# Padding the small SBUF tiles of a graph-network kernel to 128 bytes a partition

## The chip, the cores and the metric

One NeuronCore of a Trainium2 chip. The metric is the device time of one execution in microseconds (us), as the median of several executions. The kernel before takes 1516.46 us, the median of three runs from 1515.87 to 1516.89.

## The reference

A graph layer over 6250 nodes of 64 features and 200000 edges that are sorted by target node, all in float32:

```
w     = silu(edge_attr_32 @ W1 + b1) @ W2 + b2            # per edge: 32 -> 64 -> 9
h_src = x[src]                                            # per edge: a row of 64
msg   = einsum('ef,em,fmg->eg', h_src, edge_attr_9 * w, W_tp)
agg   = segment_sum(msg, dst, num_segments=6250) / sqrt(16)
gamma, beta = split(silu(node_vec[:, None] @ Wn1 + bn1) @ Wn2 + bn2, 2)
y     = x + agg * (1 + gamma) + beta
out   = (y - mean(y)) / sqrt(var(y) + 1e-5)               # over the 64 features
```

## The kernel before

Edges go in tiles of 128, one edge a partition, and 16 tiles make a group: 1563 tiles, 98 groups (`NBLK`). The loop over the groups is written out by hand under a manual schedule, so each engine gets its instructions in the order of the source. In turn `i` the kernel finishes group `i`, prepares group `i + 1` and starts on group `i + 2`.

**Source rows.** For most tiles of a group the rows `x[src]` come by indirect DMA, one for each tile, issued by POOL (`gather`, L93), six groups ahead, into one of seven `hs` buffers. Every fourth group has one tile that SP loads row by row instead (`load_rows`, L104 and L109). The last four tiles of a group (three in every fourth) need no DMA: `pick` forms their rows on TensorE. The node table stands in SBUF as `xs[0]` and `xs[1]`, two float32r halves of every value, 49 node rows a partition in seven slices of 7 x 64 numbers. A one-hot `hot_k` marks the partition and the slice of each edge's node (DVE, L479). Fourteen matmuls (seven slices, two halves) accumulate in `px` (PE, L494: stationary `hot_k[:, h]`, 128x128; moving `xs[i][:, h]`, 448 float32r a partition). DVE selects one row in seven (`xm`, L503) and sums it into `hs` (L505).

**Edge weights and sums.** `hidden` (L422, L430) and `second` (L439, L442) are the two-layer network on the edge attributes, and `weights` (L449, L455, L461) turns its result and spreads it over a window of seven nodes (`a`). `windows` (L527) multiplies rows by weights, ACT copies the result into `ztw` (L537), `project` (L573, L576, L579) multiplies by W_tp, and `place` and `bring` (L589, L595, L598, L606) add windows to nodes. `nodes` also holds the gate's matmul (L619), and `finish_nodes` (L710 to L725) the layer norm. A general path behind a flag is for other orders of edges; it is not entered with these inputs.

**SBUF.** Tiles come from pools, which lay their tiles one after the other in the order in which they are first asked for. In the program as built, every tile begins at a multiple of 32 bytes: a tile of 4 bytes a partition takes 32. So a small tile between two large ones moves the second by 32 bytes or not, by how many small ones stand ahead of it. These are the start addresses, as the remainder of a division by 64 and by 256 bytes; the offsets of the slices that the instructions address inside `xs`, `hot_k`, `ztw`, `ea`, `hs` and `c` are themselves multiples of 64:

```
tile (bytes a partition)                read or written at            before: mod 64, mod 256   after: mod 64, mod 256
ea, sh, kr, cb (first of each, loads)    L390, L392, L410, L354, L422    0, 128                      0, 0
hs (4096, seven buffers)                L93, L109, L505, L527           0, 128                      0, 0
st, p2s, a, r, c, carry, rt, yt (work)  L430 to L606                    0                           0
ident, ident2                           L449, L579, L606                0                           0
xs0, xs1 (12544 each)                   L494 moving                    32, 32                       0, 0
hot_k (3584, seven buffers)             L494 stationary, L479          32, 160                      0, 0
ztw (10240)                             L573 moving, L537              32                           0
wn2a, ht0, ht1                          L619 moving, stationary        32                           0
xm, y, sq, o                            L503, L505, L710 to L725       32                           0 (o, xm, y, sq)
gam, xb (12544 each)                    L239, L240, L710, L711         32                           0
```

Of the kernel before, what the change touches and what calls it, by code (L numbers as in the profile page):

```python
# [7 lines left out]
F32 = mybir.dt.float32  # L8
I32 = mybir.dt.int32
# [3 lines left out]
AF = mybir.ActivationFunctionType  # L13
# [3 lines left out]
P = 128  # L17
N, F, M, D, H, E = 6250, 64, 9, 32, 64, 200000
# [3 lines left out]
KB = 16  # L22
NBLK = (NT + KB - 1) // KB
W = 7
# [6 lines left out]
J = 7  # L31
# [26 lines left out]
    return min(KB, NT - g * KB)  # L58


@with_exitstack
def gnn_resnorm_kernel(ctx: ExitStack, tc: tile.TileContext, x, src, dst, dst_row, ea, sh, cn,
                       w1, b1, w2, b2, wtp, wn1, bn1, wn2, bn2, out):
    nc = tc.nc

    consts = ctx.enter_context(tc.tile_pool(name="consts", bufs=1))
# [2 lines left out]
    src_i = consts.tile([P, NBLK * KB], I32)  # L69
    dst_i = consts.tile([P, NBLK * KB], I32)  # L70
    w1bd = consts.tile([P, 2 * H], F32)
    b1c = consts.tile([P, 1], F32)
    w2bd = consts.tile([P, 2, M], F32)
    b2r = consts.tile([P, M], F32)
    wtc2 = consts.tile([P, 5, F], F32)
    flag_i = consts.tile([1, 1], I32)
    gam = consts.tile([P, NJ, F], F32)
    xb = consts.tile([P, NJ, F], F32)
    eps = consts.tile([P, 1], F32)

    with ExitStack() as fast:
        loads = fast.enter_context(tc.tile_pool(name="loads", bufs=3))
# [2 lines left out]
        keep = fast.enter_context(tc.tile_pool(name="keep", bufs=1))  # L85
# [5 lines left out]
        def gather(g):  # L91
            hs[g] = gath.tile([P, KB, F], F32, tag="hs", name=f"hs{g}")
            hs_dma[g] = [nc.gpsimd.indirect_dma_start(  # L93
                out=hs[g][:, t - g * KB, :], out_offset=None, in_=x,
                in_offset=bass.IndirectOffsetOnAxis(ap=src_i[:, t:t + 1], axis=0))
                for t in range(g * KB + (g in SPG), g * KB + tiles(g) - picked(g))]
# [14 lines left out]
        ident = keep.tile([P, P], F32)  # L111
        ident2 = keep.tile([P, F], F32)
        w2p = keep.tile([P, D], F32)
        b2c = keep.tile([P, 1], F32)
        xs = [keep.tile([P, J, F, J], F32R, name=f"xs{i}") for i in range(2)]
        wi = keep.tile([P, W], F32)
        nf = keep.tile([P, 2 * P], F32)
        lo = keep.tile([P, NBLK], F32)
        nk = keep.tile([P, J], F32)
        li = keep.tile([P, J], F32)  # L120
        ztw = keep.tile([P, 4 * 5 * KB * 8], F32)
        zt = ztw[:, 0:4 * 5 * KW].rearrange("p (a c k w) -> p a c k w", a=4, c=5, k=KB)
        rel = keep.tile([P, NBLK * KB], F32)
        nid = keep.tile([P, NBLK], F32)
        first_f = keep.tile([KB, NBLK], F32)
        bad = keep.tile([P, 4], F32)
        spare = keep.tile([P, 1], F32)
        ext = keep.tile([P, 4], F32)
        C = NBLK * Q
        jl = keep.tile([P, C], F32)  # L130
        kd = dram.tile([C, P], F16, name="kd")
        cn_d = dram.tile([P, NJ], F32, name="cn_d")
        cn_v = cn_d.rearrange("p j -> (p j)")
        wn1c = keep.tile([H, 1], F32)
        bn1c = keep.tile([H, 1], F32)
        wn2a = keep.tile([H + 1, 2 * F], F32)
        ht = [keep.tile([H + 1, 4, P], F32, name=f"ht{k}") for k in range(2)]

# [212 lines left out]
        def gate_load(j0):  # L351
            nj = min(4, NJ - j0)
            cb[j0] = loads.tile([H, 4, P], F32, tag="cb", name=f"cb{j0}", bufs=2)
            nc.sync.dma_start(cb[j0][:, :nj].rearrange("h j p -> h (j p)"), rows(cn_v[j0 * P:(j0 + nj) * P], H))  # L354
# [30 lines left out]
        def load(g, split=False):  # L385

            n = min(LB, NBLK - g)
            e = loads.tile([P, LB, KB * P // 4], F32, tag="ea", name=f"ea{g}")
            for a0, a1 in ((0, 1), (1, n)) if split else ((0, n),):
                nc.sync.dma_start(e[:, a0:a1, :], ea[g + a0:g + a1].rearrange("g p c -> p g c"))  # L390
            s = loads.tile([P, LB, KB, M], F32, tag="sh", name=f"sh{g}")
            nc.sync.dma_start(s[:, :n].rearrange("p g k m -> p g (k m)"), sh[g:g + n].rearrange("g p c -> p g c"))  # L392
            for i in range(n):
                ea_t[g + i] = e[:, i, :]
                sh_t[g + i] = s[:, i]

        def near(g):

            n = min(LB, NBLK - g)
            o = loads.tile([P, LB * KB, W], F32, tag="oh", name=f"oh{g}")  # L400
            nc.vector.tensor_tensor(
                o[:, :n * KB, :], rel[:, g * KB:(g + n) * KB].unsqueeze(2).to_broadcast([P, n * KB, W]),
                wi[:, None, :].to_broadcast([P, n * KB, W]), op=ALU.is_equal)
            for i in range(n):
                oh_t[g + i] = o[:, i * KB:(i + 1) * KB, :]

        def load_keys(g):
            n = min(LB, NBLK - g)
            kr = loads.tile([P, LB, Q, P], F16, tag="kr", name=f"kr{g}", bufs=2)
            nc.sync.dma_start(kr[:, 0:n].rearrange("p g t e -> p (g t e)"),  # L410
                              rows(kd[g * Q:(g + n) * Q, :].rearrange("c e -> (c e)"), P))
            for i in range(n):
                kr_t[g + i] = kr[:, i, Q - picked(g + i):, :]
# [56 lines left out]
        def keys(g):  # L470

            pk_t[g] = psum.tile([P, Q, P], F32, tag="r", name=f"pk{g}")
            nc.scalar.copy(pk_t[g][:, 0:picked(g), :], kr_t.pop(g))  # L473

        def hots(g, t0, t1):

            for t in range(t0, min(t1, picked(g))):
                hot_k[g, t] = late.tile([P, J, P], F32R, tag="hot_k", name=f"hot_k{g}_{t}", bufs=7)
                nc.vector.tensor_tensor(hot_k[g, t], pk_t[g][:, t, None, :].to_broadcast([P, J, P]),  # L479
                                        nk.unsqueeze(2).to_broadcast([P, J, P]), op=ALU.is_equal)  # L480
# [149 lines left out]
        with tc.manual_schedule(), tc.tile_pool(name="temp", bufs=1) as temp:  # L630
            setup(temp)

            for i in range(NBLK):
                if i + AHEAD < NBLK:
                    gather(i + AHEAD)
                while stores:
                    stores.pop(0)()
                if i % LB == 0 and i + LB < NBLK:
                    if i > 0:
                        load(i + LB)  # L640
                    near(i + LB)
                if i % LB == 1 and i + 1 + LB < NBLK:
                    load_keys(i + 1 + LB)
                if i % 4 == 3 and i + 1 < NJ:
                    gate_load(i + 1)
                for g in SPG:
                    if AHEAD - SPS < g - i <= AHEAD:
                        load_rows(g, (AHEAD - g + i) * SPR)
                more = []
                if i + 2 < NBLK:  # L650
                    keys(i + 2)
                    more = [lambda: hots(i + 2, 0, 2)]
                pick(i + 1, 0, [nodes(i), more])
                if i + 2 < NBLK:
                    hots(i + 2, 2, Q)
                if 56 <= i <= 58:
                    reach(i - 56)
                if i == 60:
                    reach_all()
                if i + 2 < NBLK:  # L660
                    hidden(i + 2)
                if i == NBLK - 2:
                    break
                second(i + 1)
                windows(i)
                turn = project(i // 2) if i % 2 == 1 else []
                if i % 4 == 1 and i - 1 < NJ:
                    gate_hidden(i - 1)
                pick(i + 1, 1, [weights(i + 1), turn])
                for t in range(2, Q):  # L670
                    pick(i + 1, t)

            g = NBLK - 1
            second(g)
            nc.scalar.activation(spare, eps, AF.Sqrt)
            pick(g, 1, [weights(g)])
            pick(g, 2)
            sums(g)
            windows(g - 1)
            pick(g, 3)  # L680
            marks(g // 2)
            turn = project(g // 2)
            windows(g, [ZT])
            ends = []
            for f in turn + place(g // 2, psum.tile([P, 2 * P], F32, tag="s", name="ps_l")):
                f()
            marks(NBLK // 2)
            for f in bring(NJ - 3, NJ - 1, psum.tile([P, FB, F], F32, tag="s", name="py_l"), ends):
                f()
            windows(g, [0])  # L690
            ends.pop()()
            project(NBLK // 2)
            ps = psum.tile([P, 2 * P], F32, tag="p1", name="ps_n")
            for f in place(NBLK // 2, ps) + bring(NJ - 1, NJ, psum.tile([P, 1, F], F32, tag="r", name="py_n")):
                f()
            while stores:
                stores.pop(0)()
# [206 lines left out]
```

## Time and profile before

| what | before |
|---|---|
| median of three runs | 1516.46 us |
| profiled execution: its own time, and its span | 1518.18 us, 1516.3 us |
| granted TensorE clock, mean of the span | 0.988 |
| PE busy | 1465.4 us, 97% |
| DVE busy | 1151.0 us, 76% |
| POOL busy | 1113.1 us, 73% |
| ACT busy | 514.3 us, 34% |
| L494, busy time of its 5138 matmuls | 1141.7 us |

The span runs from the first to the last instruction; the execution's own time has some 2 us around it. A share of busy time is an average over the whole span. The profile gives each group of instructions its source line, its operation, the tiles that it writes and reads, the count, the busy time and the mean duration of one. Matmuls are pipelined, so one that is listed with 375 ns does not hold TensorE for 375 ns: the distance from one start to the next is what it costs. The chain of waits follows the work that ended last back through the span; its pieces between two PE entries are start-to-start distances.

### The profile page before, as it was taken

How to read it: one execution, taken by the hardware profiler on the slowest of the kernel's cores; microseconds unless marked ns; L12 is line 12 of the kernel's file. 1: busy time of each engine (PE TensorE's matmuls, PEld its weight loads, DVE VectorE, ACT ScalarE, POOL GpSimd, SP SyncE). 2: the span in 40 equal slices, each digit the busy share in tenths (PEclk: the TensorE clock that was granted, in tenths of full speed). 3: DMA queues.
4: the chain of work that ended last, by engine and by line, in shares of the span. 5: the costliest groups of instructions: out<-in, count | busy, mean ns of one | idle time of the engine just before them, and what ended most of it. 6: DMA issues, size and time to landing. Idle time of an engine off the chain costs nothing.

```text
span 1516.3 us, 34381 instructions
## 1 busy us (share of the span) xinstructions
PE 1465.4 (97%) x10984; PEld 1207.4 (80%) x10984; DVE 1151.0 (76%) x2044; ACT 514.3 (34%) x1326; POOL 1113.1 (73%) x1182
## 2 busy tenths in 40 slices
PE   5899999999999999999999999999999999999996
PEld 3688788878787888787878888788888888888885
DVE  6777877778878777778687788787886877877774
ACT  3223333333333333334233324243342333333342
POOL 7777777777777777777777777777777777777760
PEclk8899999999999999999999999999999999999997
DMA  5422222222222222222222222222222222222210
GB/s 165 95 74 64 70 60 64 54 58 71 65 56 73 57 64 55 65 64 65 54 72 55 60 54 73 59 55 53 72 62 54 72 55 60 66 60 60 72 27 6
DMA packets 90424, 96.30 MB, mean 64 GB/s; under 512 B 36824, under 2 KB 51370, under 8 KB 90234
## 3 DMA queue, kind: packets, MB, share of 16 engines
q1 hardware_dynamic: 52122, 53.89, 12.0%
q0 software_dynamic: 37536, 38.51, 11.7%
q8 instruction: 90, 1.47, 0.4%
q10 hardware_dynamic: 576, 1.61, 0.3%
q14 instruction: 100, 0.82, 0.2%
HBM read 92.17 MB, written 1.73 MB: 62 GB/s over the span
## 4 chain that ended last, share of the span: by engine, by line
PE 73%; POOL 9%; DVE 5%; issue 5%; DMA 3%; ACT 3%; SPq 2%; POOLq 0%; DVEq 0%; ACTq 0%
PE px L494 55%; POOL hs L93 9%; PE pz L527 5%; PE p L422 4%; DMA hs<-in_x_dram,src_i 3%; PE pt L573 3%; PE p L439 3%; SPq L109 1%; PE p L449 1%; ACT L430 1%; ACT st L430 1%; DVE xm L503 1%; DVE hs L505 1%; PE ps L589 1%; PE ps L619 0%
## 5 line engine op out<-in xcount | busy, mean ns | idle before, releaser
L93 POOL DMA_INDIRECT hs<-in_x_dram,src_i x1173 | 1111.8, 948 | 359.6 <-issue 320.3
L494 PE MATMUL px<-xs,hot_k 128*128 128x448 f32 x5138 | 1141.7, 375 | 2.7 <-ACT xs L239 1.3
L494 PEld LDWEIGHTS px<-xs,hot_k 128*128 128x128 f32 x5138 | 929.4, 189 | 100.3 <-DVE xs L240 3.5
L503 DVE SCALAR_TENSOR_TENSOR xm<-li,jl,px 128x448 f32<-128x448 f32 x367 | 248.4, 677 | 238.6 <-PE px L494 238.6
L479 DVE TENSOR_TENSOR hot_k<-pk,nk 128x896 fp32r<-128x896 f32 x367 | 382.8, 1081 | 2.9 <-PE pk L225 2.9
L430 ACT ACTIVATE st<-p,b1c 128x1024 f32<-128x1024 f32 x98 | 109.2, 1114 | 400.5 <-PE p L422 400.2
L505 DVE TENSOR_REDUCE hs<-xm 128x64 f32<-128x448 f32 x367 | 227.6, 620 | 12.6
L537 ACT COPY ztw<-pz 64x140 f32<-64x140 f32 (+1 forms) x780 | 208.3, 267 | 16.2 <-PE pz L527 5.3
L527 PEld LDWEIGHTS pz<-a,hs 128*64 128x64 f32 x3116 | 100.0, 138 | 43.7 <-issue 42.4
L461 DVE TENSOR_TENSOR a<-oh,p 128x1008 f32<-128x1008 f32 x98 | 118.0, 1204 | 3.3
L527 PE MATMUL pz<-a,hs 128*64 128x63 f32 x3116 | 113.4, 225 | 3.2 <-DMA hs<-in_x_dram,src_i 1.9
L422 PE MATMUL p<-ea,w1bd 64*128 64x512 f32 x392 | 111.6, 646 | 0.0
L595 ACT COPY carry<-ps 128x128 f32<-128x128 f32 x48 | 12.7, 265 | 279.4 <-PE ps L589 279.4
L455 DVE TENSOR_TENSOR p<-p,sh 128x72 f32<-128x72 f32 x196 | 47.0, 240 | 58.8 <-ACT rt L576 28.1
L439 PEld LDWEIGHTS p<-st,w2p 128*32 128x32 f32 x784 | 15.8, 107 | 89.1 <-issue 43.9
L722 ACT ACTIVATE var<-var,eps 128x2 f32<-128x2 f32 (+1 forms) x25 | 7.4, 295 | 209.0 <-DVE var L719 209.0
L439 PE MATMUL p<-st,w2p 128*32 128x256 f32 x784 | 62.9, 392 | 15.2 <-DVE xb L363 7.7
L573 PE MATMUL pt<-ztw,wtc 128*64 128x112 f32 x960 | 55.2, 261 | 2.3 <-ACT st L430 2.3
L473 ACT CAST pk<-kr 128x512 f32<-128x512 f16 (+1 forms) x96 | 54.1, 564 | 1.9 <-DMA kr<-kd 1.9
L422 PEld LDWEIGHTS p<-ea,w1bd 64*128 64x128 f32 x392 | 29.7, 186 | 29.9 <-issue 26.2
L449 PE MATMUL p<-ident,p2s 128*128 128x128 f32 x196 | 53.4, 272 | 0.0
L442 ACT ACTIVATE p2s<-p,b2c 128x256 f32<-128x256 f32 x98 | 45.7, 467 | 15.7 <-PE p L439 15.7
(139 smaller groups left out, 528.7 us busy)
## 6 DMA issues: line engine op xcount, KB each, us to landing
hs<-in_x_dram SPq DMA_DIRECT2D x2944, 0.2 KB
ea<-in_ea_dram SPq DMA_DIRECT2D x48, 512.0 KB
hs<-in_x_dram,src_i POOLq DMA_INDIRECT x1173
kr<-kd SPq DMA_DIRECT2D x48, 256.0 KB
sh<-in_sh_dram SPq DMA_DIRECT2D x49, 144.0 KB
cb<-cn_d SPq DMA_DIRECT2D x12, 128.0 KB
out_dram<-o SPq DMA_DIRECT2D x24, 64.0 KB
dst_i<-in_dst_dram SPq DMA_DIRECT2D x1, 768.0 KB
```

The source lines that it names most:

```text
L93: hs_dma[g] = [nc.gpsimd.indirect_dma_start(out=hs[g][:, t - g * KB, :], out_offset=None, in_=x, in_offset=bass.IndirectOffsetOnAxis(ap=sr ...
L422: nc.tensor.matmul(p1[:, i, :], w1bd[i * 64:(i + 1) * 64, :], e[i * 64:(i + 1) * 64, :], start=True, stop=True)
L430: nc.scalar.activation(st[g], p1_t.pop(g), AF.Silu, bias=b1c)
L439: nc.tensor.matmul(p2[g][c * D:(c + 1) * D, 0, :].rearrange("p (i e) -> p i e", i=2), w2p, s[:, :, c * P:(c + 1) * P], start=True, stop=True)
L461: nc.vector.tensor_mul(a[g], oh_t.pop(g)[:, :, None, :].to_broadcast([P, KB, M, W]), sw.unsqueeze(3).to_broadcast([P, KB, M, W]))
L479: nc.vector.tensor_tensor(hot_k[g, t], pk_t[g][:, t, None, :].to_broadcast([P, J, P]), nk.unsqueeze(2).to_broadcast([P, J, P]), op=ALU.is_ ...
L494: nc.tensor.matmul(px.rearrange("p f l -> p (f l)"), hot_k[g, t][:, h, :], xs[i][:, h].rearrange("p f l -> p (f l)"), start=(h == 0 and i ...
L503: nc.vector.scalar_tensor_tensor(xm, li[:, None, :].to_broadcast([P, F, J]), jl[:, c:c + 1], px, op0=ALU.is_equal, op1=ALU.mult)
L505: nc.vector.tensor_reduce(hs[g][:, tiles(g) - q + t, :], xm, AX.X, ALU.add)
L527: mm = nc.tensor.matmul(pz[v][v * F:(v + 1) * F, k // 2].rearrange("p m w -> p (m w)"), hsg[:, k0 + k, :], ag[:, k0 + k].rearrange("p m w ...
L537: nc.scalar.copy(z[h * F:(h + 1) * F, 0:5 - h, k0 + v:k0 + n:2, :].rearrange("p m k w -> p k m w"), pz[v][v * F:(v + 1) * F, 0:(n + 1 - v) ...
L573: nc.tensor.matmul(pt[h * F:(h + 1) * F, 0, 0:KW], wtc2[:, c, :], z[h][:, c], start=(c == 0), stop=(c == 4))
```

## The change

A helper rounds the free size of a tile up to 32 numbers of four bytes, 128 bytes, and hands back the part that was asked for. It is used for the small tiles and for those whose size is no multiple of 128 bytes. One tile is given another name (`spare` becomes `root`). The instructions, their order on every engine, their shapes and their semaphore waits stay as they are; what differs is the address at which tiles begin, as in the table above, and that the tiles end some 1.6 KB higher in SBUF.

```diff
+def even(pool, p, n, dt, **kw):
+
+    per = 32
+    return pool.tile([p, -(-n // per) * per], dt, **kw)[:, 0:n]
+
...
-    b1c = consts.tile([P, 1], F32)
-    w2bd = consts.tile([P, 2, M], F32)
-    b2r = consts.tile([P, M], F32)
+    b1c = even(consts, P, 1, F32, name="b1c")
+    w2bd = even(consts, P, 2 * M, F32, name="w2bd").rearrange("p (s m) -> p s m", s=2)
+    b2r = even(consts, P, M, F32, name="b2r")
     wtc2 = consts.tile([P, 5, F], F32)
-    flag_i = consts.tile([1, 1], I32)
+    flag_i = even(consts, 1, 1, I32, name="flag_i")
     gam = consts.tile([P, NJ, F], F32)
     xb = consts.tile([P, NJ, F], F32)
-    eps = consts.tile([P, 1], F32)
+    eps = even(consts, P, 1, F32, name="eps")
...
-        b2c = keep.tile([P, 1], F32)
+        b2c = even(keep, P, 1, F32, name="b2c")
         xs = [keep.tile([P, J, F, J], F32R, name=f"xs{i}") for i in range(2)]
-        wi = keep.tile([P, W], F32)
+        wi = even(keep, P, W, F32, name="wi")
         nf = keep.tile([P, 2 * P], F32)
-        lo = keep.tile([P, NBLK], F32)
-        nk = keep.tile([P, J], F32)
-        li = keep.tile([P, J], F32)
+        lo = even(keep, P, NBLK, F32, name="lo")
+        nk = even(keep, P, J, F32, name="nk")
+        li = even(keep, P, J, F32, name="li")
         ztw = keep.tile([P, 4 * 5 * KB * 8], F32)
...
```

The same is done to `rel`, `nid`, `first_f`, `bad`, `root`, `ext`, `jl`, `wn1c` and `bn1c`, which stand behind `ztw` and ahead of `wn2a`, `ht` and the pool that holds `hot_k`, `xm` and the tiles of the layer norm.

More of the change, by code (lines that the diff above doesn't have):

```diff
@@ L113, in gnn_resnorm_kernel @@
         w2p = keep.tile([P, D], F32)
-        b2c = keep.tile([P, 1], F32)
+        b2c = even(keep, P, 1, F32, name="b2c")
         xs = [keep.tile([P, J, F, J], F32R, name=f"xs{i}") for i in range(2)]
-        wi = keep.tile([P, W], F32)
+        wi = even(keep, P, W, F32, name="wi")
         nf = keep.tile([P, 2 * P], F32)
-        lo = keep.tile([P, NBLK], F32)
-        nk = keep.tile([P, J], F32)
-        li = keep.tile([P, J], F32)
+        lo = even(keep, P, NBLK, F32, name="lo")
+        nk = even(keep, P, J, F32, name="nk")
+        li = even(keep, P, J, F32, name="li")
         ztw = keep.tile([P, 4 * 5 * KB * 8], F32)
         zt = ztw[:, 0:4 * 5 * KW].rearrange("p (a c k w) -> p a c k w", a=4, c=5, k=KB)
[L123 to L128, printed above, removed]
+        rel = even(keep, P, NBLK * KB, F32, name="rel")
+        nid = even(keep, P, NBLK, F32, name="nid")
+        first_f = even(keep, KB, NBLK, F32, name="first_f")
+        bad = even(keep, P, 4, F32, name="bad")
+        root = even(keep, P, 1, F32, name="root")
+        ext = even(keep, P, 4, F32, name="ext")
         C = NBLK * Q
-        jl = keep.tile([P, C], F32)
+        jl = even(keep, P, C, F32, name="jl")
         kd = dram.tile([C, P], F16, name="kd")
@@ L133, in gnn_resnorm_kernel @@
         cn_v = cn_d.rearrange("p j -> (p j)")
-        wn1c = keep.tile([H, 1], F32)
-        bn1c = keep.tile([H, 1], F32)
+        wn1c = even(keep, H, 1, F32, name="wn1c")
+        bn1c = even(keep, H, 1, F32, name="bn1c")
         wn2a = keep.tile([H + 1, 2 * F], F32)
@@ L674, in gnn_resnorm_kernel @@
             second(g)
-            nc.scalar.activation(spare, eps, AF.Sqrt)
+            nc.scalar.activation(root, eps, AF.Sqrt)
             pick(g, 1, [weights(g)])
```

## The prediction

> **What bounds the kernel now.** The first part of the page, then the chain of waits, then the table by stretches, then the costliest groups.
>
> ```profile
> PE 1465.4 (97%) x10984; PEld 1207.4 (80%) x10984; DVE 1151.0 (76%) x2044; ACT 514.3 (34%) x1326; POOL 1113.1 (73%) x1182
> PE px L494 55%; POOL hs L93 9%; PE pz L527 5%; PE p L422 4%; DMA hs<-in_x_dram,src_i 3%; PE pt L573 3%; PE p L439 3%; SPq L109 1%; PE p L449 1%; ACT L430 1%; ACT st L430 1%; DVE xm L503 1%; DVE hs L505 1%; PE ps L589 1%; PE ps L619 0%
> ```
>
> ```profile
> 200.00:800.00 600.00, 590.33 (x4500) 489.21 (x4499) 462.98 (x837) 209.67 (x540) 453.58 (x481) 1.00 0.24 63
> 800.00:1480.00 680.00, 674.74 (x5112) 557.20 (x5111) 525.94 (x892) 234.58 (x610) 509.17 (x539) 1.00 0.23 59
> ```
>
> The second fence gives, for two stretches, their length and then the busy time of PE, weight loads, DVE, ACT and POOL, the granted clock, the DMA share and GB/s. TensorE works 98.4% and 99.2% of them at the full clock, so in the loop its own instructions are the time. Of PE's 50.9 us without work (1516.3 - 1465.4) the larger part lies ahead of 50 us and behind 1480 us. POOL is the second bound: the groups list 1111.8 us for its 1173 gathers, and 320.3 us between them in which it waits for nothing, so it issues one in about 1.25 us without a break. Its records run from 4.0 to 1473.3 us, and the last group's gathers are needed by L527 at 1496.8: it has 23.5 us to spare there.
>
> Everything thus hangs on whether an address changes the time of an instruction, above all of L494's. With 5138 of them, 0.59 ns in one is 0.2% of the time (3.0 us), about what a measurement of this kernel can tell from no change.
>
> **What L494 costs, and whether its address is in it.** The chain's pieces around the loop's other matmuls (start, length, count):
>
> ```profile
> 802.36 0.82 PE px L494 x4
> 803.18 0.22 PE ps L619 x2
> 803.40 0.41 PE px L494 x2
> 803.81 0.12 PE ps L589
> 803.93 0.42 PE px L494 x2
> 804.35 0.12 PE ps L589
> 804.47 1.64 PE px L494 x8
> ...
> 792.72 0.96 PE pt L573 x20
> 793.68 0.61 PE px L494 x2
> 794.29 0.11 PE p L449
> ...
> 796.13 0.11 PE pt L579
> ```
>
> From the start times of the matmul records, over 97 undisturbed runs of L494, one takes 204.0 ns; the shortest run's mean is 203.7, the longest's 204.3. The Trainium skill, "TensorE: Matmul & The Clock Gate", section Back-to-back issue gap, prices a matmul in a stream at columns/2.4 + 2.5 ns: 189.2 ns for 448 columns. This trace doesn't agree; it shows 14.8 ns more. Two operands of L494 begin 32 bytes behind a multiple of 64 (`xs`, `hot_k`), which is what the change ends, so the 14.8 ns are the question. Three comparisons inside this one trace answer it:
>
> 1. **L589 is an aligned float32r matmul**: moving `c`, 256 columns, stationary `r`, both already at multiples of 64. From the start of the L494 ahead of it to an L494 behind it, less 204.0 for each L494, it costs 124.4 ns as the mean of 95. The page's price is 109.2; it pays 15.2 ns more, as L494 does, though it is aligned. The surplus is a fixed one per float32r matmul: neither the address nor the length is in it.
> 2. **L619 is an unaligned float32 one**: `wn2a` and `ht` both 32 behind. Its two records take 0.22 us, 0.11 for each 128x128. The aligned L449 and L579 take 0.11 for their one record of 128x128. L573 streams the unaligned `ztw`: 20 records in 0.96 us, 48 ns for each 112 columns, with two output halves side by side; 96 ns for a pair, where L449's 110 ns for 128 columns make 96 for 112.
> 3. **The stationary operand**: a weight load of `hot_k` takes 189 ns, of the aligned `w1bd` (L422) 186 and `r` (L589) 187, all beside a matmul. An L494 beside which `r` is loaded goes on to the next start after 203.4 ns, no faster than beside `hot_k`.
>
> "SBUF — State Buffer", section Specifications (TRN2), says that a line of SBUF is 16 bytes and that each cross to a new line has a price. Starts 0 and 32 behind a multiple of 64 both lie on such a line, so 1792 bytes are 112 lines either way. Its section Operand start alignment says that its measurements there are of legality and timed nothing. No run here shows the lines as such; comparisons 1 and 2 are what I build on.
>
> **The change part by part.** It adds and removes no instruction, no DMA and no wait on any queue, SP's and POOL's among them. Nothing is queued behind anything new. What moves is addresses:
>
> - *xs, hot_k (L494, 5138 matmuls and loads).* 5138 x 0 = 0 by comparisons 1 and 3. As a bound, aligned L589 pays 15.2 ns and unaligned L494 14.8: 0.4 ns more is +2.1 us. My reading of L589 is good to 1 to 2 ns, which is some 5 to 10 us of doubt to both sides if one trusted nothing else.
> - *ztw (960 records), wn2a and ht (98 records): PE.* 0 by comparison 2.
> - *hot_k, xm, y, xb on DVE.* The rows:
>
> ```profile
> L479 DVE TENSOR_TENSOR hot_k<-pk,nk 128x896 fp32r<-128x896 f32 x367 | 382.8, 1081 | 2.9 <-PE pk L225 2.9
> L505 DVE TENSOR_REDUCE hs<-xm 128x64 f32<-128x448 f32 x367 | 227.6, 620 | 12.6
> L461 DVE TENSOR_TENSOR a<-oh,p 128x1008 f32<-128x1008 f32 x98 | 118.0, 1204 | 3.3
> L713 DVE TENSOR_REDUCE mean<-y 128x2 f32<-128x128 f32 x24 | 6.9, 286 | 0.8
> L576 ACT COPY rt<-pt 128x112 f32<-128x112 f32 x48 | 12.1, 253 | 3.5 <-PE pt L573 2.4
> L537 ACT COPY ztw<-pz 64x112 f32<-64x112 f32 x389 | 99.1, 255 | 4.5
> ```
>
>   L505 and L713 (both read 32 behind) give (620 - 286)/(448 - 128) = 1.044 ns a number and 152 ns fixed. That makes 1204 for L461, whose SBUF tiles are all aligned: it shows 1204. For L479, which writes 32 behind, it makes 1087; it shows 1081, less. No price of the address, so 0. DVE stands idle a quarter of the time anyway; where PE waits for it (L439 for `xb`, 7.7 us in all), nothing shortens.
> - *ztw on ACT.* L576 writes an aligned tile in 253 ns, L537 the same 112 numbers 32 behind in 255. 2 ns x 780 copies = 1.6 us on an engine that is busy a third of the span: 0.
> - *The setup (L239, L240: gam to xs, seven each, 963 and 928 ns).* They are on the chain at 13 us. Both read with a stride of 64 numbers, aligned or not. L224 writes `xb` 32 behind in 330 ns where L187 writes the aligned `ident` in 287: 43 ns x 7 = 0.3 us. I take 0; bounds -2 and +1 us.
> - *DMA destinations.* `hs`, `ea`, `kr` were at multiples of 64 and stay so, but go from 128 behind a multiple of 256 to 0 behind. "DMA: Bandwidth & Descriptors", section How a descriptor splits into AXI transactions, has a descriptor that doesn't start at a multiple of 256 fetch from the boundary below, one transaction more. If that held for destinations, a 256-byte row of `hs` would land in one transaction rather than two; no run here shows it. The cover is the six groups of lead: PE waited for gathers 2.7 us in all, 1.9 at matmuls and 0.8 at weight loads. Bound 0 to -2.7, taken 0.[...]
>
> Sum: 1516.3 + 0 for the profiled span, whose execution took 1518.18, 1.7 above the median of the runs. Against the median of 1516.46 I forecast **1516.5 us**.
>
> **The rivals.**
>
> *Faster: L494's surplus is the address after all*, and L589 pays its own for another reason (its weights change beside it, say). All 14.8 ns gone would be 76 us. If only the 29th piece of 64 bytes goes (1792 bytes that begin 32 behind touch 29 such pieces, aligned ones 28; my supposition), it is 16 columns, 6.7 ns, 34 us. Either would meet POOL's pace: the last gather is issued at 1473.3 and has landed within 4 us (the chain's longest such wait is 3.70), and 19.5 us follow L527's 1496.8. So the end can't come before 1496, and both give about **1496 us**. One cycle of 2.4 GHz each would be 2.1 us, two 4.3. Against it stand comparisons 1 to 3. Faster by over 0.2%: 0.18, half of it by small amounts.
>
> *Slower: everything now starts at the same place.* `xs` stood 32 and `hot_k` 160 behind a multiple of 256; after it, both are at 0, and so are `hs` and `xm`, which other engines write. If TensorE's two reads, or a read and a DVE write, got in each other's way for equal remainders, each L494 would pay. It decides from 0.59 ns; two cycles of 2.4 GHz, 0.83 ns, are 4.3 us: **1520.8 us**. The price of a whole piece of 64 bytes would be 34 us, 1551, and no other engine hides that. For it speaks only that aligned L589 is 0.4 ns dearer; against it that the loop's L494 are 204.0 whatever DVE and ACT do beside them. 0.14.
>
> *The change doesn't do what it says.* The built program's addresses show that it does: `xs`, `hot_k`, `ztw`, `xm` and `wn2a` now start at multiples of 64; `hs`, `a`, `ea` did so before.
>
> **How the numbers follow.** No effect: 0.68, within 0.2%, 1513.4 to 1519.5. The range adds the small cases, four cycles of 2.4 GHz to the fast side and two to the slow: 1508 to 1521; out stay the large ones. Chances: faster 0.18, same 0.68, slower 0.14.
>
> **What would show it right or wrong.** Right: L494's start-to-start distance stays at 204 ns (20 of them 4.08 us in the chain), L573's 20 records at 0.96 us, L479 at 1081 and POOL's at 948 ns. The fast rival shows 40 L494 in less than the 8.15 us of now, POOL or DMA taking a larger part of the chain, and PE's share falling; the slow one shows them in more, at a granted clock of 1.00. A change in DVE's rows alone should leave the time as it is.

## The result and the profile after

The changed kernel takes **1511.93 us** (median of 11 runs) against 1516.89 for the one before (11 runs beside them): a ratio of 0.9968 with a 95% interval from 0.9959 to 0.9978. It is faster by 0.32%, where no change was forecast. Its profiled execution took 1512.09 us with a span of 1510.2, 6.1 us less than the span before. (The execution profiled before took 1518.18 us, 1.3 above the median of its eleven, so the two spans lie further apart than the medians, which differ by 5.0.)

The page after, in the order of the lines shown of before: busy time by engine, the chain by line, and the two stretches of the loop.

```profile
PE 1459.4 (97%) x10984; PEld 1207.7 (80%) x10984; DVE 1152.7 (76%) x2044; ACT 514.6 (34%) x1326; POOL 1113.2 (74%) x1182
PE px L500 63%; PE pz L533 6%; PE p L428 5%; PE p L445 3%; PE pt L579 3%; POOL hs L99 2%; SPq L115 1%; PE p L455 1%; ACT L436 1%; DMA hs<-in_x_dram,src_i 1%; ACT st L436 1%; DVE xm L509 1%; PE ps L595 1%; DVE hs L511 1%; PE ps L625 1%
```

```profile
200.00:800.00 600.00, 590.29 (x4512) 491.46 (x4511) 464.38 (x835) 209.57 (x539) 453.49 (x481) 1.00 0.24 63
800.00:1480.00 680.00, 674.31 (x5130) 559.02 (x5129) 529.08 (x895) 235.90 (x613) 509.23 (x539) 1.00 0.23 59
```

PE's busy time fell by 6.0 us, nearly all of the span's 6.1; no other engine's did. TensorE's share of the two stretches is what it was, and so is its clock, but it gets more done: 5130 matmul records in the second against 5112. So TensorE's instructions follow each other more closely. (Lines after are six higher: L494 is now L500.)

Which ones, the chain says. Here are two neighbouring stretches of L494 in the kernel before, then the same two after; start, length, count:

```profile
1194.62 10.61 PE px L494 x52
1211.48 6.94 PE px L494 x34
```

```profile
1189.41 10.53 PE px L500 x52
1206.18 6.88 PE px L500 x34
```

52 matmuls take 0.08 us less, 1.5 ns each. From the start times in the 97 unbroken runs of at least 20 L494 (without the first five distances of each), one goes to the next in 202.63 ns, against 204.08. By contrast these rows, which could have shown a price of alignment, are as they were:

```profile
L485 DVE TENSOR_TENSOR hot_k<-pk,nk 128x896 fp32r<-128x896 f32 x367 | 382.7, 1081 | 1.9 <-PE pk L231 1.9
L511 DVE TENSOR_REDUCE hs<-xm 128x64 f32<-128x448 f32 x367 | 227.6, 620 | 12.6
L500 PEld LDWEIGHTS px<-xs,hot_k 128*128 128x128 f32 x5138 | 929.7, 189 | 93.5 <-DVE xs L246 3.2
L99 POOL DMA_INDIRECT hs<-in_x_dram,src_i x1173 | 1111.9, 948 | 359.5 <-issue 316.9
```

DVE's one-hot 1081 ns, its sum 620, the weight load 189, POOL's gather 948: all equal to before. One row of DVE did change: `c` (L557, now L563) takes 372 ns in place of 360, 1.2 us in all on an engine with time to spare. The addresses of its own tiles aren't the reason: aligned_128, a kernel further down in which they are as after, has 359.

5138 matmuls at 1.45 ns make 7.4 us. The loop keeps 5.4 of them: from group 1's first L422 record to group 97's it took 1436.5 us before and 1431.1 after. Some go at the joints. An L449 between two L494 costs some 111 ns in place of 109 (196 of them, about 0.5 us; the figure shifts by a few ns with the start behind it to which one measures), and the block of L422, L439, L527 and L573 costs 4243 ns in place of 4233 (47, another 0.5). The rest, in the short runs of two L494 between other matmuls, was not taken apart. The profile after also reaches group 1 1.1 us earlier. The granted clock switches at other moments of the first 50 us there; with the ratio's interval of 0.2%, nothing more is read from it.

### The profile page after: what moved, and what is told of

It is laid out like the page before. It is cut to its first block, busy times and chain, and to the rows that moved or that the text cites. A ratio compares the mean times of both kernels' runs of the same rounds, so it can differ in the third digit from the quotient of the medians.

```text
span 1510.2 us, 34381 instructions
## 1 busy us (share of the span) xinstructions
PE 1459.4 (97%) x10984; PEld 1207.7 (80%) x10984; DVE 1152.7 (76%) x2044; ACT 514.6 (34%) x1326; POOL 1113.2 (74%) x1182
## 4 chain that ended last, share of the span: by engine, by line
PE 84%; DVE 6%; ACT 2%; issue 2%; SPq 2%; POOL 2%; DMA 1%; DVEq 0%; POOLq 0%; ACTq 0%
PE px L500 63%; PE pz L533 6%; PE p L428 5%; PE p L445 3%; PE pt L579 3%; POOL hs L99 2%; SPq L115 1%; PE p L455 1%; ACT L436 1%; DMA hs<-in_x_dram,src_i 1%; ACT st L436 1%; DVE xm L509 1%; PE ps L595 1%; DVE hs L511 1%; PE ps L625 1%
## 5 line engine op out<-in xcount | busy, mean ns | idle before, releaser
L500 PE MATMUL px<-xs,hot_k 128*128 128x448 f32 x5138 | 1136.1, 374 | 2.0 <-ACT xs L245 1.3
L500 PEld LDWEIGHTS px<-xs,hot_k 128*128 128x128 f32 x5138 | 929.7, 189 | 93.5 <-DVE xs L246 3.2
L485 DVE TENSOR_TENSOR hot_k<-pk,nk 128x896 fp32r<-128x896 f32 x367 | 382.7, 1081 | 1.9 <-PE pk L231 1.9
L579 PEld LDWEIGHTS pt<-ztw,wtc 128*64 128x64 f32 x960 | 46.8, 137 | 4.6 <-ACT st L436 4.0
```

The source lines that it names most:

```text
L500: nc.tensor.matmul(px.rearrange("p f l -> p (f l)"), hot_k[g, t][:, h, :], xs[i][:, h].rearrange("p f l -> p (f l)"), start=(h == 0 and i ...
L579: nc.tensor.matmul(pt[h * F:(h + 1) * F, 0, 0:KW], wtc2[:, c, :], z[h][:, c], start=(c == 0), stop=(c == 4))
```

## Which tile's address: four kernels

Theories at this point: **A**, the stream of `xs` pays for a start off a multiple of 64; **B**, the weight load of `hot_k` pays and holds the stream; **C**, what counts is how the two lie to each other; **D**, another tile or the DMA destinations. Each kernel is the changed one with one thing put back inside a tile made larger, so that no other tile changes its remainder by 64:

```diff
-        xs = [keep.tile([P, J, F, J], F32R, name=f"xs{i}") for i in range(2)]
+        XO = (8, 8)             # xs32, both32: 32 bytes; xs64: (16, 16); hot32: (0, 0)
+        xs = [keep.tile([P, J * F * J + 64], F32R, name=f"xs{i}")[:, XO[i]:XO[i] + J * F * J]
+              .rearrange("p (h f l) -> p h f l", h=J, f=F) for i in range(2)]
...
-                hot_k[g, t] = late.tile([P, J, P], F32R, tag="hot_k", name=f"hot_k{g}_{t}", bufs=7)
+                hot_k[g, t] = late.tile([P, J * P + 16], F32R, tag="hot_k", name=f"hot_k{g}_{t}", bufs=7)[
+                    :, 8:8 + J * P].rearrange("p (j e) -> p j e", j=J)      # hot32, both32 alone
```

In their first run every kernel, the one before too, took some 2530 us: the profile of xs32 shows DVE held up for 541 us by what it can only name as remote, and TensorE's granted clock falling to 0.82 on the mean. What held DVE up was not found. These times say nothing of addresses; only the distances inside stretches without a halt could be used. So the four were run again on another chip.

xs32: 

> The changed kernel with both xs tiles put back to 32 bytes behind a multiple of 64 (inside larger tiles, so nothing else changes its remainder by 64); hot_k, ztw, hs and all others stay aligned. Theory A, the moving stream of L494 pays for its own start: L494's start-to-start distance goes back from 202.6 to 204.0 ns and the time to some 1517 us. Theory B, the weight load of hot_k pays and holds the stream up: 202.6 ns, 1512 us. Theory C, both must be aligned, or share a remainder: between them or 204. Theory D, the DMA destinations (now multiples of 256) or another tile are behind it: 202.6 and 1512.

hot32: 

> The changed kernel with the hot_k buffers alone put back to 32 bytes behind a multiple of 64; xs stays aligned. Theory A: 202.6 ns for an L494, 1512 us. Theory B: 204.0 ns, 1517 us. Theory C: between them or 204. Theory D: 202.6 and 1512. The weight load's own duration stays near 189 ns in all of them, since it was 189 in both kernels.

both32: 

> The changed kernel with xs and hot_k both put back to 32 behind a multiple of 64, all other tiles aligned. Theories A, B and C: 204.0 ns for an L494 and the time before, 1517 us. Theory D: 202.6 ns and 1512 us.

xs64: 

> The changed kernel with both xs tiles 64 bytes behind a multiple of 256: still a multiple of 64, no longer one of 128 or 256. Theory A with 64 bytes as the unit, theory B and theory D: 202.6 ns and 1512 us. If the unit is 128 bytes or more, or if equal remainders of xs and hot_k matter (theory C): a different distance, 203 to 204 ns, 1514 to 1517 us.

In that first run L494's distance was some 206 ns in xs32, 204 in hot32, 203 in both32 and 200 in xs64, as means of few stretches. Already these don't fit A or B: xs32 lies above the kernel before, and xs64 below the one after. The second run, with the kernel before at 1516.96 us:

xs32_b: 

> The same kernel as xs32 (changed kernel, both xs tiles 32 bytes behind a multiple of 64), on a chip where the kernel before is near 1517 us. In the run of xs32 every kernel took some 2530 us, with TensorE stopped for other reasons; its undisturbed stretches had L494 distances of 200.0, 204.3 and 206.7 ns, most of them 206.7. Theory A (the moving stream pays for its start): 204 to 206.7 ns here, 1517 to 1533 us. Theory B (the weight load pays): 202.6 and 1512. Theory C (what counts is how the two reads fall against each other): any of 200.0, 204.3 or 206.7, and one alone through the whole loop.

hot32_b: 

> The same kernel as hot32 (changed kernel, hot_k alone 32 bytes behind a multiple of 64). In hot32's stretches: 200.0, 203.4, 205.0 and 206.7 ns. Theory A: 202.6 ns, 1512 us. Theory B: 204.0 and 1517. Theory C: one of the four, another than 202.6.

both32_b: 

> The same kernel as both32 (changed kernel, xs and hot_k 32 behind, all else aligned). All theories that put the gain on these two tiles: 204.0 ns and 1517 us, as before the change. If it stays at 202.6 and 1512, another tile's address is behind the gain.

xs64_b: 

> The same kernel as xs64 (changed kernel, xs 64 bytes behind a multiple of 256, hot_k at one). In xs64's stretches every L494 took 200.0 ns. Theories A and B, with 64 bytes as the unit: 202.6 ns and 1512 us. Theory C: 200.0 ns, 5138 x 2.6 = 13 us less than the changed kernel, some 1499 us.

| kernel | xs, hot_k by the remainder of 256 | L494 start to start, ns | us | ratio to before, interval |
|---|---|---|---|---|
| before | 32, 160 | 204.08 | | |
| after | 0, 0 | 202.63 | 1511.93 | 0.9968 (0.9959 to 0.9978) |
| xs32_b | 32, 0 | 206.43 | 1529.39 | 1.0084 (1.0067 to 1.0101) |
| hot32_b | 0, and 32, 96, 160 or 224 by buffer | 204.39 | 1520.57 | 1.0020 (1.0012 to 1.0028) |
| both32_b | 32, and 32, 96, 160 or 224 by buffer | 202.71 | 1513.78 | 0.9976 (0.9969 to 0.9982) |
| xs64_b | 64, 0 | 200.05 | 1506.23 | 0.9923 (0.9906 to 0.9939) |

xs64_b has the distance that was expected, but not the 1499 us: part of the gain is given back around the other matmuls (the last section has numbers). The chain of xs32_b and then of xs64_b shows the two ends, as long stretches of L494:

```profile
1203.09 10.73 PE px L502 x52
```

```profile
1186.23 10.41 PE px L502 x52
```

A alone falls: putting `xs` back makes the kernel slower than before, and putting both back leaves most of the gain. B alone falls: moving `xs`, with `hot_k` in place, moves the time by 23 us. By its expectation both32_b speaks for D, another tile. But it doesn't bring the old distance back: its longer buffers, and those of hot32_b, lie 3648 bytes apart, so the picks go through four distances in place of the one, 128, of before. Theory D therefore stays open here and is settled by the next two kernels.

Sorted by `hot_k` less `xs`, by the remainder of 256 bytes, the values suggest something else: 0 gives 202.6, 128 gives 204.1, 192 gives 200.0, 224 gives 206.4. The two kernels with four distances can be split by buffer. Over the last six distances of each pick (those without a break), both32_b has 203.1, 202.1, 204.0 and 200.0 ns at 0, 64, 128 and 192; hot32_b has 204.2, 205.3 and 206.1 at 32, 160 and 224. That is theory **E**: the distance in bytes counts, the alignment doesn't.

The distance alone doesn't fix the time of every run, though. At 96, hot32_b has two values: of 87 picks 51 go at 200.0 and 28 at 206.7 ns. And the 206.43 of xs32_b, always at 224, is a mean: 83 of its 97 long runs go at 206.7, 13 at 204.6, and one, which began after a halt, at 200.0, all from the same addresses. Two runs of 20 in its chain:

```profile
890.60 4.12 PE px L502 x20
...
1014.54 4.09 PE px L502 x20
```

So a distance allows more than one pattern. That the way in which a run begins picks one of them is likely, but wasn't tested. In before, after and xs64_b all 97 runs lie within 0.6 ns of their mean.

## The distance alone

**Aligned, at the old distance.** The changed kernel, with an unused tile ahead of `hot_k`:

```diff
         ht = [keep.tile([H + 1, 4, P], F32, name=f"ht{k}") for k in range(2)]
+        gap = keep.tile([P, 32], F32, name="gap")
```

> The changed kernel with an unused tile of 128 bytes ahead of hot_k: every large tile still begins at a multiple of 64, but hot_k begins 128 bytes behind xs by the remainder of 256, as it did before the change (there 160 against 32). Theory E (only the distance from xs to hot_k by the remainder of 256 counts; seen so far: 0 gives 202.6 ns, 128 gives 204.0, 192 gives 200.0, 224 gives 206.4): 204.0 ns for an L494 and the time before, 1517 us, with everything aligned. Theory A (the multiples of 64 are what helps): 202.6 ns and 1512 us.

Measured: 203.99 ns, 1518.51 us against 1517.84, ratio 1.0005 (0.9996 to 1.0014).

**Unaligned, at another distance.** The kernel before, with the same line and 16 numbers in place of 32:

> The kernel before with one unused tile of 64 bytes ahead of hot_k and nothing else: xs still begins 32 behind a multiple of 64, hot_k too, but the distance by the remainder of 256 is 192 in place of 128. Theory E: 200.0 ns for an L494, 5138 x 4.0 = 20.6 us less in those matmuls, some 1.5 to 2 us a hundred of it given back around the others as in the run of xs64_b: 1506 us, faster than the changed kernel although nothing is aligned. Theory A: 204.0 ns and 1517 us, since no remainder by 64 changes.

Measured: 200.03 ns, 1506.13 us against 1517.84, ratio 0.9926 (0.9909 to 0.9942). The chains of aligned_128 and before_gap64:

```profile
1193.76 10.61 PE px L501 x52
1210.60 6.93 PE px L501 x34
```

```profile
1184.85 10.42 PE px L495 x52
1201.49 6.81 PE px L495 x34
```

The aligned kernel has the 10.61 of before and the whole gain is gone; the unaligned one beats the changed kernel. The padding's 64-byte starts thus bought nothing that these runs can tell from zero, and D falls too: in aligned_128 the other padded tiles stand as in the changed kernel, but for those behind `hot_k`, which the kernels of the next section move. What brought the 0.32% is that the padding happened to move `hot_k` from 128 to 0 behind `xs`. Here too part is given back: 4.05 ns x 5138 are 20.8 us, PE's busy time fell by 12.1.

**The whole circle.** The kernel before, with the one-hot moved 16 bytes further inside a longer buffer after each sixteenth of the picks:

```diff
-                hot_k[g, t] = late.tile([P, J, P], F32R, tag="hot_k", name=f"hot_k{g}_{t}", bufs=7)
+                o = 4 * ((4 * g + t) * 16 // (4 * NBLK))
+                hot_k[g, t] = late.tile([P, J * P + 64], F32R, tag="hot_k", name=f"hot_k{g}_{t}", bufs=7)[
+                    :, o:o + J * P].rearrange("p (j e) -> p j e", j=J)
```

> The kernel before with hot_k buffers 256 bytes longer; the one-hot is put 16 bytes further behind the buffer's start after each sixteenth of the picks, so the distance from xs to hot_k passes 128, 144, ... 368 (that is 112) in one run. Theory E: the L494 distance by sixteenths takes the values seen before where the distance is one of 0, 64, 96, 128, 192, 224 (202.6, about 202, 202.8, 204.0, 200.0, 206.4 ns) and shows the others; it says whether the step is of 16 or of 32 bytes. Theory A: every value but those at multiples of 64 from the start of hot_k is worse or the same, 204 ns and above.

From the start times, within runs of L494, in the one execution that was made (some 160 to 210 distances for each place; the means are good to some 0.2 ns):

```
hot_k - xs, mod 256:    0     16     32     48     64     80     96    112
ns:                 202.6  206.7  203.9  202.2  202.1  203.4  200.0  204.1
hot_k - xs, mod 256:  128    144    160    176    192    208    224    240
ns:                 204.1  204.0  205.4  203.4  200.1  204.4  206.1  202.9
```

Four of the places in its chain, at 128, 192, 224 and 96:

```profile
53.69 10.61 PE px L496 x52
...
415.79 8.02 PE px L496 x40
...
596.56 8.26 PE px L496 x40
...
1342.36 8.01 PE px L496 x40
```

Forty matmuls take 8.02 us at 192 and 8.26 at 224. The step of 16 bytes matters: 80, 96 and 112 give 203.4, 200.0 and 204.1. 96 is no multiple of 64 and is as good as 192 in this run, though hot32_b shows that it can also go at 206.7; 16 is the worst with 224. For 96 the expectation had 202.8 and missed. Here too some means hide two patterns: at 240 four runs have 203.3 ns and one 200.0, at 32 some have 203.3 and others 204.4. Smaller steps were not tried.

## Which two accesses

With `hot_k`, every tile behind it moved too. DVE writes `hot_k` and `xm` while TensorE reads `xs`, so the distance could be one between DVE's writes and TensorE's reads. Two kernels set them apart: all L494 take their weights from a fixed tile `hw`, while DVE goes on writing to the `hot_k` buffers at a distance of their own.

```diff
+        gap1 = keep.tile([P, 16], F32, name="gap1")         # fixed192 alone
+        hw = keep.tile([P, J, P], F32R, name="hw")
+        gap2 = keep.tile([P, 48], F32, name="gap2")         # fixed128: 16
...
-                    nc.tensor.matmul(px.rearrange("p f l -> p (f l)"), hot_k[g, t][:, h, :],
+                    nc.tensor.matmul(px.rearrange("p f l -> p (f l)"), hw[:, h, :],
```

Both also write `hw` once, with the first one-hot, and have six `hot_k` buffers. They leave out that each pick uses its own one-hot, and with it L494's wait for DVE.

fixed192: 

> The kernel before, but all matmuls of L494 take their weights from one fixed tile, hw, written once with the first one-hot; DVE goes on writing every one-hot to the hot_k buffers, which nothing reads (so the rows that pick forms are those of the first one-hot, not of each edge). hw lies 192 behind xs by the remainder of 256, the hot_k buffers that DVE writes lie 128 behind, as before. Theory F (the two reads of TensorE, stream and weights, fall against each other): 200.0 ns for an L494, some 1506 us. Theory G (what counts is where DVE writes hot_k, or xm, against where TensorE reads xs): 204.0 ns, 1517 us.

fixed128: 

> The same with the places changed over: hw lies 128 behind xs, the hot_k buffers that DVE writes 192 (and xm with them). The same part is left out. Theory F: 204.0 ns for an L494, some 1517 us. Theory G: 200.0 ns, some 1506 us.

Measured: fixed192 200.03 ns, 1507.12 us, ratio 0.9927 (0.9898 to 0.9956); fixed128 204.08 ns, 1519.10 us, ratio 1.0001 (0.9991 to 1.0011). The chains, fixed192 first:

```profile
1186.70 10.42 PE px L500 x52
```

```profile
1196.96 10.61 PE px L499 x52
```

L494's time follows `hw`, which TensorE reads, and not the buffers that DVE writes; fixed128 has the time of before, so what is left out doesn't count. What matters is thus how the two tiles lie that TensorE itself reads, the moving rows of `xs` and the weights. A weight load's listed duration is no guide to it: it stays at 189 or 190 ns from 200.0 to 206.4, while the matmuls stand closer or wider apart. The Trainium skill, "TensorE: Matmul & The Clock Gate", section Step-by-step: what each phase is for, gives TensorE two independent read ports for the two operands. These runs show that in time the two are not independent. That one read holds up the other is the likeliest reading; what inside SBUF or the engine does it was not shown.

## Why the prediction was wrong, point by point

- **The bound** was right: TensorE's instructions are the time, and the change that can be traced is in L494. The measured 1511.93 us lies inside the range, on the side that was given 0.18.
- **The step that failed is the term "5138 x 0 = 0 by comparisons 1 and 3".** It should have read 5138 x -1.45 ns = -7.4 us. What the comparisons show is true as far as it goes: alignment to 64 costs nothing that can be told, and aligned_128 confirms it with a ratio of 1.0005. But I took "no price of the alignment" for "no price of the address". The surplus of 14.8 ns over the page's price had been asked only whether it comes from a remainder by 64, of one operand at a time. Some 4 of them do depend on addresses, of two operands together (204.08 against 200.0), and no aligned L589 can show that: it has a distance of its own. The other 10.8 stay at every distance. They may be no surplus at all: the Trainium skill, "TensorE: Matmul & The Clock Gate", section Back-to-back issue gap, calls the formula of the price that of an isolated matmul, and says that in a stream of weight loads and matmuls both set the spacing.
- **Comparison 3 was too weak.** That an L494 goes on after 203.4 ns beside the load of `r` was one matmul among others. The starts behind each joint show that a run takes a few matmuls to fall into its pattern, so a single different load needn't show its effect. In xs32_b, for one, the distances behind a joint begin with 201 and 202 before they settle at 206 and 207.
- **The bound was not used.** I wrote that my reading of L589 is good to 1 to 2 ns, 5 to 10 us, and still gave the effect zero with 0.68. The measured 1.45 ns lies within that doubt, and the reading was looser than I thought: taken to the first L494 start behind it, L589 costs 119.4 ns, to the second 127.2.
- **The fast rival** had the wrong mechanism (a 29th piece of 64 bytes, whose 6.7 ns would have been 34 us). Only its small amounts, "two cycles of 2.4 GHz, 4.3 us", came near the size.
- **The slow rival** had named the right pair, TensorE's two reads by their remainder of 256, and the move from 32 and 160 to 0 and 0. It took equal remainders for the bad case. They give 202.6 ns, a middling value; 224 and 16 are the bad ones. No row of the trace before could order the distances, so its sign was a guess, and a wrong one.
- **The other zeros held as far as can be seen:** `ztw` (L573's 20 records 0.96 us again), DVE's rows but for `c`, ACT's and POOL's. For the DMA destinations no time to landing is on record; PE's waits for gathers are 1.2 us after, 2.7 before, and between 1.2 and 5.4 in the four kernels built from before, where `hs` lies as it did.
- **POOL's floor** of 1496 us was not reached by any kernel here; before_gap64 at 1506 stays above it.

## What to carry to other kernels

When an edit changes nothing but addresses, compare the start-to-start distance of the commonest matmul, to a tenth of a nanosecond, before and after. For a stream of float32r matmuls with a new weight load each (448 columns is the one shape measured here), place the stationary tile and the moving tile by their distance and try a few: one unused tile of 64 bytes gave 0.74% here, more than twice what padding 19 tiles gave. And a tile added anywhere ahead of one of the two can take as much away: compare a change with the distance held, or the change is credited with it.

## What the runs showed of the hardware that I had not expected

- A float32r matmul of 448 columns, with a 128x128 weight load for each, takes from 200.0 to 206.7 ns by where its two operands lie to each other, 3.3%, with 16 bytes of shift enough to go from 200.0 to 204.1. At some distances it has two or three values from the same addresses (224: 206.7, 204.6 and once 200.0).
- Runs of such matmuls fall into a fixed pattern of starts. Before, it repeats every five: 200, 209, 196, 204, 211 ns, 1020 in all; after, 203, 202, 203, 199, 206, 1013 in all. At 192 it repeats every three, 201, 197, 202. The same five come in the long runs before, though DVE, ACT and DMA do different things beside them.
- In these kernels a faster pattern costs more at the joints: an L449 between two L494 costs some 109 ns before, 111 after and 125 in xs64_b. It takes back a part of each gain that the distance brings: of the 20.7 us that 4.03 ns make in xs64_b, 10.7 remain in the time.
